# One scaled maximum for two heads: a VectorE multiply and one ScalarE add in place of two ScalarE operations

## The chip, the cores and the metric

The kernel runs on one core of one Trainium2 chip. A core has engines that run side by side, each with its own queue worked off in order: TensorE (PE in the profile; its weight loads are PEld), VectorE (DVE), ScalarE (ACT), GpSimd (POOL) and SyncE (SP), which only starts transfers. The metric is the device time of one execution in microseconds (us). Lower is better.

## What is computed

The program is a two-layer decoder on 16 x 128 = 2048 tokens of width 256: in each layer a self-attention, a cross-attention and a feed-forward part, each followed by a layer norm. The change touches the cross-attention of layer 0 alone. There all 2048 queries attend to all 2048 context rows in 16 heads of dimension 16, and queries, keys, values and the attention weights are rounded to 8 bits:

```python
def _fq_unsigned(x, axis):
    s = jnp.max(x, axis=axis, keepdims=True) / 255.0
    s = jnp.maximum(s, 1e-08)
    q = jnp.clip(jnp.round(x / s), 0.0, 255.0) * s
    return x + jax.lax.stop_gradient(q - x)
...
q = _fq_sym(q, axis=-1)
k = _fq_sym(k, axis=-1)
v = _fq_sym(v, axis=2)
attn = jnp.einsum('bhqd,bhkd->bhqk', q, k)
attn = jax.nn.softmax(attn.astype(jnp.float32), axis=-1)
attn = _fq_unsigned(attn, axis=-1)
out = jnp.einsum('bhqk,bhkd->bhqd', attn, v)
```

The largest weight of a row is that of its largest score. So the 8-bit weight of a score is the rounded value of 255 exp(scale (score - maximum)), which is exp(scale x score + (ln 255 - scale x maximum)). The bracket is one number per query and head. It is this number that the change computes in another way.

## The kernel before

The stage is called joint here because two things run in it together: the cross-attention of layer 0, and, two groups behind it, the feed-forward part of layer 0 for token tiles whose attention is done.

**Steps.** The list `steps` (L1117) has 128 entries (gp, i, u): eight groups gp of two query tiles of 128 tokens, in each group eight head pairs i, for each pair the two tiles u. A group is thus 16 steps. A step takes 128 queries, two heads and 2048 keys. The loop at L1123 runs over the steps, each in two parts, and the order of instructions on PE, DVE, ACT and POOL is the order in which the program writes them (`manual_schedule`, L1122).

**One step, engine by engine.** PE multiplies queries by keys (`scores`, L788), four times two matmuls of 512 keys, into PSUM tiles `s` of which there are two. DVE reads each 128 x 512 block once (`scaled`, L795): it copies the scores into the SBUF tile `e` (four buffers, two a step) and at the same time gives their running maximum; the last of its four entries for a head, `mx[:, 3, hh]`, is the maximum over all 2048 keys for head hh of the pair. That is eight DVE operations a step. ACT then forms the per-query bias of both heads (`exponent`, L812, into the tile `snl`), and one step later writes the 8-bit weights of 2048 keys with one Exp for each head (`weights8`, L827), which reads `e`, the bias from `snl` and the positive scale `qs`. PE turns the weights round, four bytes as one fp32 word (`words_T`, L840, into `aTp`); ACT or DVE copies them to SBUF (`words_out`, L846: by DVE in part 0, by ACT in part 1); POOL spreads the bytes into bf16 (`spread`, L850); PE multiplies them by the values (`context`, L863) in slices that are placed in later steps.

**The scales.** `qs` and its negative `qneg` hold one column for each of the 16 heads of a query tile. POOL computes both in `query_scale` (L616, L618), several steps before the tile's first step.

**The order inside part 1 of step n on the two engines.** DVE: four reductions of step n, then whatever was put off to this place (`due(at, "DVE")`: additions to the residual L899, norm statistics L137 and L138, the query maximum L610 and L612). ACT: copies put off to "ACT first" (L987, L165, L1007), the Exp of head 1 of step n - 1, the copy of the turned words, the feed-forward's tanh and copy (`ffn_out`, L949 and L950), and last `exponent` of step n. The Exp of head 0 of step n follows in part 0 of step n + 1, after the "ACT first" copies of that part where there are any.

**Around it.** Feed-forward matmuls (`ffn_gate` L931, `ffn_down` L966), the query projection of the next group (`query`, L991 to L1007: PE L603, DVE L610 and L612, POOL L616 to L628, PE L635, ACT L1007), and the output projection (L896) are placed at fixed steps of each group by `pair_work` (L1072) and `unit` (L1065). They share one PSUM bank, `misc`.

Of the kernel before, what the change touches and what calls it, by code (L numbers as in the profile page):

```python
# [18 lines left out]
F32 = mybir.dt.float32  # L19
# [3 lines left out]
AF = mybir.ActivationFunctionType  # L23
ALU = mybir.AluOpType
# [3 lines left out]
P = 128  # L28
# [20 lines left out]
def decoder(ctx: ExitStack, tc: tile.TileContext, w: dict, out: bass.AP):  # L49
    nc = tc.nc  # L50

    const = ctx.enter_context(tc.tile_pool(name="const", bufs=1))
    stat = ctx.enter_context(tc.tile_pool(name="stat", bufs=4))
# [157 lines left out]
    with ExitStack() as ph:  # L211
# [14 lines left out]
        wts, bias = {}, {}  # L226
# [291 lines left out]
        states, cks = {}, {}  # L518
# [68 lines left out]
    with ExitStack() as ph:  # L587
# [50 lines left out]
        qs, qneg = {}, {}  # L638
# [127 lines left out]
        ln255 = pool.tile([P, 1], F32, name="ln255")  # L766
# [10 lines left out]
        def group(gp):  # L777
            ssum = stat.tile([P, 2, 16], F32, tag="ssum", name="ssum", bufs=3)
            groups[gp] = ([], ssum)
# [11 lines left out]
        def scaled(gp, i, u, half, c, st, s):  # L791

            quarter = 2 * half + c
            for hh in range(2):
                nc.vector.tensor_scalar(  # L795
                    st["e"][hh][:, half, c * G : (c + 1) * G],
                    s[:, hh, :],
                    1.0,
                    None if quarter == 0 else st["mx"][:, quarter - 1, hh : hh + 1],
                    ALU.mult,  # L800
                    ALU.max,
                    accum_out=st["mx"][:, quarter, hh : hh + 1],
                )
# [4 lines left out]
        def exponent(gp, i, u, st):  # L808

            st["nm"] = stat.tile([P, 2], F32, tag="snl", name="snl")  # L810
            for hh in range(2):
                nc.scalar.activation(  # L812
                    st["nm"][:, hh : hh + 1],
                    st["mx"][:, 3, hh : hh + 1],
                    AF.Identity,
                    bias=ln255,
                    scale=qneg[2 * gp + u][:, 2 * i + hh : 2 * i + hh + 1],
                )

        def weights8(gp, i, u, hh, st):  # L820

# [15 lines left out]
        def words_T(hh, st):  # L837
            pt = ps.tile([P, 4, P], F32, tag="tp", name="aTp", bufs=2)
            for b in range(4):
                nc.tensor.transpose(pt[:, b, :], st["a"][hh][:, b * P : (b + 1) * P], ident)  # L840
            return pt

        def words_out(hh, st, pt, copy):

            at = wk.tile([P, 4, P], F32, tag="at", name="at", bufs=3)
            copy(at.bitcast(U16), pt.bitcast(U16))  # L846
            st["at"][hh] = at
# [126 lines left out]
        states, aTs, os = {}, {}, {}  # L974
# [7 lines left out]
        def later(at, engine, f, *args):  # L982
            put_off.setdefault((at, engine), []).append((f, args))

        def due(at, engine):
            for f, args in put_off.pop((at, engine), []):
                f(*args)  # L987
# [130 lines left out]
        states, aTs, os = {}, {}, {}  # L1118
# [3 lines left out]
        with tc.manual_schedule(engines=set(ordered)):  # L1122
            for n in range(len(steps) + 9):  # L1123
                now = steps[n] if n < len(steps) else None
                if now is not None:
                    if n % 16 == 0:
                        group(n // 16)
                    if n < NB:
                        nc.gpsimd.tensor_tensor(xs[n], xs[n], bp, ALU.add)
                    states[n] = {  # L1130
                        "e": [wk.tile([P, 2, 2 * G], F32, tag="e", name="e", bufs=4) for _ in range(2)],
                        "mx": stat.tile([P, 4, 2], F32, tag="smx", name="smx"),
                        "a": [],
                        "at": {},
                    }
                for part in range(2):
                    at = 2 * n + part
                    if now is not None:
                        if at == 0:
                            waiting = scores(*now, 0, 0)  # L1140
                        scaled(*now, part, 0, states[n], waiting)
                        scaled(*now, part, 1, states[n], scores(*now, part, 1))
                    due(at, "DVE")
                    m = n - 2 + part
                    due(at, "PE")
                    for hh in range(2):

                        q = n - 3 if (n - 3) % 2 == 1 else n - 4
                        turn = (2 * (n - q) + part, hh)

                        if hh == 1 and 0 <= m < len(steps):
                            pt = words_T(1 - part, states[m])
                        if hh == 1 and at + 1 < 2 * len(steps):
                            waiting = scores(*steps[(at + 1) // 2], (at + 1) % 2, 0)
                        if 0 <= q < len(steps) and turn in turns:
                            gp, i, _ = steps[q]
                            if turn == (7, 0) and i % 4 == 0:
                                os[gp, i // 4] = ps.tile([P, 2 * P], F32, tag="o", name="o")
                            o = os[gp, i // 4]
                            context(i, range(*turns[turn]), aTs[gp, i], o)  # L1160
                            if turn == (9, 1):
                                aTs.pop((gp, i))
                                if i % 4 == 3:
                                    later(
                                        at + 1,
                                        "ACT first",
                                        nc.scalar.copy,
                                        ot[:, i // 4],
                                        os.pop((gp, i // 4)).rearrange("p (u q) -> p u q", u=2),
                                    )  # L1170
                                if i == 7 and gp < LAST:
                                    later(at, "DVE last", sums, gp)
                                    for u in range(2):
                                        later(at + 1, "POOL", by_dim, gp, u)
                    if part == 1:
                        unit(n, 1, at)
                    due(at, "ACT first")

                    if 0 <= n - 1 < len(steps):
                        weights8(*steps[n - 1], part, states[n - 1])  # L1180
                    if 0 <= m < len(steps):
                        words_out(1 - part, states[m], pt, nc.scalar.copy if part else nc.vector.tensor_copy)
                    due(at, "ACT")
                    if 0 <= n - 2 < len(steps):
                        gp, i, u = steps[n - 2]
                        if part == 0 and u == 0:
                            aTs[gp, i] = wk.tile([P, NB, 2, 2 * P], BF16, tag="aT", name="aT")
                        due(at, "POOL first")
                        spread(u, part, states[n - 2], aTs[gp, i])
                    due(at, "POOL first")  # L1190
                    due(at, "POOL")
                    if now is not None and part == 1:
                        exponent(*now, states[n])
                    due(at, "DVE last")
                    if (n, part) == (len(steps), 1):
                        later(at + 1, "DVE", sums, LAST)
                        for u in range(2):
                            later(at + 2, "POOL", by_dim, LAST, u)
                    if n < len(steps):
                        pair_work(n, bool(part))  # L1200
                    else:
                        tail_work(n, bool(part))
                if n == len(steps) + 3:
                    ffn_load_all()
                states.pop(n - 3, None)
            assert not put_off, put_off

            for i in range(NI):
                for n in range(2):
                    ffn_gate(LAST, i, n, "s")  # L1210
                th, gu = ffn_tiles(LAST, i, tail=True)
                ffn_out(LAST, th, gu)
                ffn_sigmoid(th, nc.vector)
                ffn_mult(LAST, i, th, gu, nc.vector)
            exp_tables()
            for u in range(2):
                ffn_put_out(LAST, range(NI * u, NI * u + NI), 0, "s")
                due(1, "DVE")
            due(1, "POOL")
            due(2, "POOL first")  # L1220
# [199 lines left out]
    with ExitStack() as ph:  # L1420
# [53 lines left out]
        with tc.manual_schedule(engines={mybir.EngineType.PE, mybir.EngineType.Activation}):  # L1474
# [6 lines left out]
            for h in range(len(halves) + 8):  # L1481
# [16 lines left out]
                if 0 <= h - 2 < len(halves):  # L1498
                    u, d = halves[h - 2]
# [19 lines left out]
    with ExitStack() as ph:  # L1519
# [51 lines left out]
        with tc.manual_schedule(engines={mybir.EngineType.PE}):  # L1571
# [8 lines left out]
            for n in range(len(steps) + 14):  # L1580
# [15 lines left out]
                if 0 <= n - 3 < len(steps):  # L1596
                    u, c = steps[n - 3]
# [135 lines left out]
```

## Time and profile before

| what | value |
|---|---|
| time before, median of 3 runs | 2814.71 us (2813.69 to 2815.48) |
| the profiled execution: its own time | 2814.12 us |
| span of its trace | 2812.4 us |
| joint stage, first to last reduction at L795 | 867.0 to 1718.2 us |
| L812, two to a step | x256, 89.2 us busy, median 392 ns |
| L827, two to a step | x256, 534.8 us busy, mean 2098 ns |
| L795, eight to a step | x768 of mean 745 ns, x256 of mean 682 ns |
| mean granted PE clock | 0.969 |

The profile page has a row for each engine over the span in 40 slices of 70 us; a digit is the busy share in tenths. The joint stage lies in the 13th to 25th slice, and in it DVE and ACT stand at 9 almost throughout while PE stands at 8. Durations of neighbouring instructions of DVE and ACT overlap a little, so the cost of one in a full queue is better read from start to start in the timeline. A busy share over the stage also hides that the stage has stretches with different limits. The page's first table gives for the whole program PE 91%, DVE 72%, ACT 59%, POOL 44%.

### The profile page before, as it was taken

What the parts mean: (1) busy time and instruction counts of PE and PEld (TensorE: products, weight loads), DVE (VectorE), ACT (ScalarE), POOL (GpSimd) and SP (SyncE); (2) the same over time, 40 slices, a digit from 0 to 9 for tenths busy, and PEclk for the clock granted to TensorE, in tenths of its full rate; (3) what the DMA queues carried; (4) which work ended last, traced back from release to release, by engine and by line L of the source; (5) the groups of instructions that cost most, each with busy time, mean ns of one, the idle gap of its engine ahead of it and who ended that gap; (6) DMA issues with size and microseconds to landing.
All of it is one profiled execution on the core that took longest, in us unless ns stands there. A gap on an engine that the chain in (4) does not pass through costs nothing.

```text
span 2812.4 us, 45068 instructions
## 1 busy us (share of the span) xinstructions
PE 2557.1 (91%) x15957; PEld 1594.8 (57%) x15988; DVE 2017.6 (72%) x5525; ACT 1672.6 (59%) x3178; POOL 1236.6 (44%) x1390
## 2 busy tenths in 40 slices
PE   6999999999987788888888888899988899999998
PEld 3677777777753344444444445565655555565646
DVE  5877878777759999999999995577867753333232
ACT  2566566666637999989999996455555442223120
POOL 6544444444446777877778776323322200000000
PEclk9999999999996899999999999999999999999999
DMA  8000000000010000100000001400010011111120
GB/s 242 3 1 1 1 1 1 1 1 1 1 38 10 1 12 20 29 12 22 24 14 26 20 16 51 148 2 2 2 52 12 4 48 58 42 49 53 38 64 12
DMA packets 85009, 79.71 MB, mean 28 GB/s; under 512 B 19728, under 2 KB 66288, under 8 KB 84272
## 3 DMA queue, kind: packets, MB, share of 16 engines
q1 hardware_dynamic: 83520, 73.41, 8.6%
q0 software_dynamic: 1264, 3.42, 0.6%
q8 instruction: 127, 2.08, 0.3%
q14 instruction: 98, 0.80, 0.1%
HBM read 74.57 MB, written 2.23 MB: 27 GB/s over the span
## 4 chain that ended last, share of the span: by engine, by line
PE 66%; DVE 13%; ACT 10%; issue 5%; POOL 4%; DMA 1%; SPq 0%; ACTq 0%; DVEq 0%; POOLq 0%
PE proj L377 11%; PE gate L1641 6%; PE py L1672 6%; PE up L1641 6%; DVE e L795 6%; PE po L507 4%; ACT a L827 4%; PE gu L931 3%; PE o L863 2%; PE sc L423 2%; PE o L1360 2%; PE s L788 2%; PE pm L495 2%; PE aTp L840 2%; PE pm L494 2%
## 5 line engine op out<-in xcount | busy, mean ns | idle before, releaser
L850 POOL CAST aT<-at 128x2048 bf16<-128x2048 uint8 x256 | 482.9, 1893 | 176.0 <-ACT at L846 100.4
L795 DVE TENSOR_SCALAR_CACHE_REDUCE e<-s,smx 128x512 f32<-128x512 f32 x768 | 535.6, 745 | 23.7 <-PE s L788 20.9
L827 ACT ACTIVATE a<-e,snl,qs 128x2048 uint8<-128x2048 f32 x256 | 534.8, 2098 | 0.0
L788 PE MATMUL s<-kT,qT 64*128 64x512 bf16 x1024 | 212.1, 409 | 68.8 <-DVE e L795 67.1
L840 PE MATMUL aTp<-ident,a 128*128 128x128 f32 x1024 | 178.3, 299 | 34.9 <-ACT a L827 34.7
L1645 DVE TENSOR_TENSOR h<-h,up 128x512 f32<-128x512 f32 (+1 forms) x100 | 68.8, 688 | 192.7 <-PE up L1641 191.4
L1644 ACT ACTIVATE h<-gate 128x512 f32<-128x512 f32 (+1 forms) x100 | 59.7, 597 | 220.5 <-PE gate L1641 220.2
L863 PE MATMUL o<-aT,vq 128*32 128x256 bf16 x2048 | 189.4, 289 | 0.0
L795 DVE TENSOR_SCALAR_CACHE_REDUCE e<-s 128x512 f32<-128x512 f32 x256 | 167.1, 682 | 27.6 <-PE s L788 22.1
L1351 ACT COPY prT<-tp 128x512 f32<-128x512 f32 x192 | 104.8, 587 | 123.6 <-PE tp L1350 123.2
L840 PEld LDWEIGHTS aTp<-ident,a 128*128 128x128 f32 x1024 | 114.4, 148 | 99.7 <-ACT a L827 58.6
L1641 PE MATMUL gate<-xT,w_L_ffn_w1g 128*128 128x512 f32 x352 | 167.7, 595 | 0.0
L788 PEld LDWEIGHTS <-qT 64*128 64x128 bf16 x1024 | 56.9, 93 | 194.3 <-issue 193.9
L1641 PE MATMUL up<-xT,w_L_ffn_w1u 128*128 128x512 f32 x352 | 165.4, 592 | 0.0
L1672 PE MATMUL py<-w_L_ffn_w2T,h 128*128 128x256 f32 x704 | 154.6, 379 | 0.0
L846 ACT COPY at<-aTp 128x1024 uint16<-128x1024 uint16 x128 | 129.2, 1010 | 33.8 <-PE aTp L840 32.4
L1316 POOL TENSOR_TENSOR vz<-v,ones 128x1024 f32<-128x1024 f32 (+1 forms) x32 | 58.6, 1831 | 201.1 <-ACT v L1453 83.9
L1339 DVE TENSOR_REDUCE amx<-sc 128x8 f32<-128x1024 f32 x96 | 116.5, 1216 | 38.9 <-PE sc L1331 38.7
L1672 PEld LDWEIGHTS py<-w_L_ffn_w2T,h 128*128 128x128 f32 x704 | 133.7, 190 | 18.3
L377 PE MATMUL proj<-Wlk,xT 128*128 128x512 f32 x256 | 123.7, 606 | 7.4 <-DMA Wlk<-in_L_attn_Wlk 6.3
L447 ACT ACTIVATE pls<-sc,lm,rms_rs 128x128 f32<-128x128 f32 x256 | 113.8, 454 | 25.7 <-DVE lm L443 25.7
L931 PE MATMUL gu<-xT,wgu 128*128 128x256 f32 x448 | 126.6, 405 | 2.4 <-ACT gu_s L950 2.2
(317 smaller groups left out, 5977.8 us busy)
## 6 DMA issues: line engine op xcount, KB each, us to landing
wgu<-in_L_ffn_gu SPq DMA_DIRECT2D x112, 128.0 KB
sh<-share SPq DMA_DIRECT2D x32, 256.0 KB
sh<-share SPq DMA_DIRECT2D x16, 224.0 KB
sh<-share SPq DMA_DIRECT2D x16, 192.0 KB
w_L_ffn_w1g<-in_L_ffn_w1g SPq DMA_DIRECT2D x1, 2816.0 KB
w_L_ffn_w1u<-in_L_ffn_w1u SPq DMA_DIRECT2D x1, 2816.0 KB
w_L_ffn_w2T<-in_L_ffn_w2T SPq DMA_DIRECT2D x1, 2816.0 KB
sh<-share SPq DMA_DIRECT2D x16, 160.0 KB
```

The costliest lines, as they stand in the source:

```text
L377: nc.tensor.matmul(pp.rearrange("p h d -> p (h d)"), lhsT=xTt(b, k), rhs=wts[nm, hg][:, k, :], start=k == 0, stop=k == 1)
L788: nc.tensor.matmul(s[:, hh, :], lhsT=qT[t % 4][r, i, :], rhs=kT[r, i, at : at + G], start=True, stop=True)
L795: nc.vector.tensor_scalar(st["e"][hh][:, half, c * G : (c + 1) * G], s[:, hh, :], 1.0, None if quarter == 0 else st["mx"][:, quarter - 1, ...
L827: nc.scalar.activation(a.bitcast(U8), st["e"][hh].rearrange("p a b -> p (a b)"), AF.Exp, bias=st["nm"][:, hh : hh + 1], scale=qs[2 * gp + ...
L840: nc.tensor.transpose(pt[:, b, :], st["a"][hh][:, b * P : (b + 1) * P], ident)
L846: copy(at.bitcast(U16), pt.bitcast(U16))
L850: nc.gpsimd.tensor_copy(aT[:, :, hh, u * P : (u + 1) * P].rearrange("p (b j) q -> p b j q", j=4), st["at"].pop(hh).bitcast(U8).rearrange(" ...
L863: nc.tensor.matmul(o[r : r + 32], lhsT=vq[:, n, h // 2, h % 2 : h % 2 + 2].rearrange("p w d -> p (w d)"), rhs=aT[:, n, hh], start=n == 0 a ...
L931: nc.tensor.matmul(ffn_ps[q][:, n, :], lhsT=wt[:, k, :], rhs=xT[q // 2][:, k, at], start=k == 0, stop=k == 1)
L1339: nc.vector.tensor_reduce(mx, sc, AX.X, ALU.max)
L1641: nc.tensor.matmul(pp[:rows], lhsT=wt[:, k, :], rhs=xT[g][:, k, :], start=k == 0, stop=k == 1)
L1672: nc.tensor.matmul(py, lhsT=h[:rows, i4 * P : (i4 + 1) * P], rhs=wt, start=n == 0, stop=n == len(parts) - 1)
```

## The change

The multiplication by the negative scale moves from ACT to DVE. DVE does it for both heads in one operation on 128 x 2 numbers, straight after the last reduction of a step and ahead of what was put off to that place. ACT then adds ln 255 to both heads' products in one operation whose scale is a plain number. A new tile `smq` (four buffers) carries the products.

```diff
         def exponent(gp, i, u, st):
 
             st["nm"] = stat.tile([P, 2], F32, tag="snl", name="snl")
-            for hh in range(2):
-                nc.scalar.activation(
-                    st["nm"][:, hh : hh + 1],
-                    st["mx"][:, 3, hh : hh + 1],
-                    AF.Identity,
-                    bias=ln255,
-                    scale=qneg[2 * gp + u][:, 2 * i + hh : 2 * i + hh + 1],
-                )
+            nc.scalar.activation(st["nm"], st["mq"], AF.Identity, bias=ln255)
+
+        def scaled_max(gp, i, u, st):
+            st["mq"] = stat.tile([P, 2], F32, tag="smq", name="smq")
+            nc.vector.tensor_tensor(st["mq"], st["mx"][:, 3, :], qneg[2 * gp + u][:, 2 * i : 2 * i + 2], ALU.mult)
...
                         scaled(*now, part, 1, states[n], scores(*now, part, 1))
+                        if part == 1:
+                            scaled_max(*now, states[n])
                     due(at, "DVE")
```

No matmul and no transfer is added or taken away. The count of ACT operations falls by 128 (256 to 128), that of DVE operations rises by 128.

## The prediction

> **What bounds the kernel now.** I read the page's rows first, then the groups of DVE and ACT instructions, then the chain that ended last, the timeline and the windows. The groups:
>
> ```profile
> L827 ACT ACTIVATE a<-e,snl,qs 128x2048 uint8<-128x2048 f32 x256 | 534.8, 2098 | 0.0
> ...
> L812 ACT ACTIVATE snl<-smx,ln,qneg 128x1 f32<-128x1 f32 x256 | 89.2, 397 | 13.7 <-DVE e L795 13.3
> ...
> L103 ACT ACTIVATE nrs<-nss,eps 128x1 f32<-128x1 f32 x32 | 9.4, 294 | 0.8
> ...
> L443 DVE TENSOR_TENSOR lm<-lm,rms_rs 128x4 f32<-128x4 f32 x64 | 10.4, 162 | 0.0
> ```
>
> The reader is to see the operation that goes (L812), and the two rows nearest to what comes: an ACT operation with a pointer bias but a plain scale (L103, 294 ns), and a small DVE product (L443, 162 ns).
>
> A bare step needs about 5.6 us of ACT and 5.9 us of DVE, so neither wins everywhere. From the third group of steps on, every group takes 109.22 us (for instance 1184.73 to 1293.95 between the same L812), and the chain changes engine inside it. Two pieces of the chain, both from the group that starts at 1184.7:
>
> ```profile
> 1190.37 0.40 ACT th L949
> 1190.76 0.47 ACT gu_s L950
> 1191.23 0.56 ACT snl L812 x2
> 1191.79 2.08 ACT a L827 x2
> 1193.92 0.66 PE aTp L840 x4
> ...
> 1228.99 1.42 DVE e L795 x5
> 1230.41 0.34 DVE x L899
> 1230.78 0.44 DVE ln_st L137
> ```
>
> In the first, ACT sets the pace and the 0.56 us of the L812 pair lies on the chain. In the second, DVE does, and anything put after its eighth reduction lies on the chain. I walked through one group and counted. On the chain are **five L812 pairs** (those at 1266.4, 1272.9, 1286.8, and the two like 1184.9 and 1191.2) and **five ends of a step's reductions on DVE** (1208.4, 1216.1, 1223.5, 1230.4, 1250.5). The rest of the group's chain is PE work, the POOL query rounding and other DVE work.
>
> The first two groups have less PE work: from 867 to 1015 the chain is almost all DVE and passes 19 ends of steps. After the last group's slow PE stretch, from 1688 to 1721, ACT never idles and the chain is ACT alone, with six more pairs.
>
> **The change on ACT.** In the timeline the L812 pair starts at 1191.09 and the Exp behind it at 1191.66, so a pair holds ACT for 0.57 us. The new single operation has one pointer fewer; by the L103 row it lasts 0.295 us. What it holds depends on what follows. If an independent copy follows (L1007, L165 or L987), neighbours overlap: the copy at 1189.46 lasts 1.01 and the next starts at 1190.35, so 0.11 is hidden and the operation holds 0.185; saving 0.385. If the Exp follows directly it reads this very result. Before, it read what the *first* of the pair wrote while the second covered the delay. The row for a result read at once is this:
>
> ```profile
> 1873.42 0.29 ACT L103 ACTIVATE ln_rstd<-ln_mv,eps 128x4 f32<-128x4 f32 x1
> 1873.75 0.20 ACT L104 ACTIVATE ln_rstd<-ln_rstd 128x4 f32<-128x4 f32 x1
> ```
>
> No overlap, 0.33 from start to start; saving 0.24. The Trainium skill ("ScalarE: Activation LUTs", What ACT_TABLE_LOAD costs) prices each pointer operand at about 93 ns, as the rows do, and says that neighbouring ACTIVATEs overlap by about 93 ns, without an exception for a dependent one. By the rule all five pairs of a group save about 0.38, 1.9 us; by the rows it is 3 x 0.24 + 2 x 0.385 = **1.49 us**. I take the rows. If the new operation keeps the old 0.39 us, the saving is 0.98.
>
> **The change on DVE.** The product has no row of its own size; L443 at 162 ns is nearest. It reads what the accumulator read just wrote, and no row shows that wait. Now the next instruction starts together with the read (both at 1230.37). Low end: no wait, 0.16 less the overlap of 0.08: 0.08. Between: read 0.08, a gap of 0.04 as between L137 and L138 (1208.80 + 0.43, then 1209.27), then 0.16, less 0.08: 0.20. High: no overlap afterwards, 0.28. I take **0.20**, as L138 is a dependent small operation of the same engine. Five on a group's chain: 1.0 us. Behind the product in DVE's queue stand the residual additions of L899 and the reductions of the next step; PE waits for both (psum `misc` and `s`).
>
> **The added wait.** ACT now waits for the product, not the maximum, so it gets the bias about 0.2 us later. In the ACT-bound steps DVE has finished 1.4 to 3.4 us before L812 starts, so this is free. In the three or four steps of a group where L812 waits for DVE, ACT idles 0.8 to 1.8 us later in the same step for PE, which itself waits for DVE; that is the cover, and without it the cost would be 0.2 us a step. `qneg` is ready well ahead.
>
> **Sum along the old chain.** First two groups: 19 x 0.20 = +3.8, less 0.4 for one pair; six periods of 1.0 - 1.49 = -0.49: -2.9; the end: 4 x 0.24 + 2 x 0.385 = -1.7. Together -1.2 us, under 0.05%.
>
> **The clock ties this sum.** The granted clock halves once in each group, for two windows of 3.41 us:
>
> ```profile
> 1216.16:1219.57 3.41, 2.06 (x16) 1.00 0.01 2
> ...
> 1229.81:1233.22 3.41, 1.51 (x12) 1.00 0.00 0
> 1233.22:1236.64 3.42, 2.58 (x14) 0.50 0.00 0
> 1236.64:1240.05 3.41, 3.41 (x19) 0.50 0.00 0
> 1240.05:1243.46 3.41, 3.41 (x26) 1.00 0.00 1
> ...
> 1260.53:1263.94 3.41, 1.89 (x20) 1.00 0.13 38
> ```
>
> The columns are the stretch, its length, PE busy with its instructions, and the clock. After a window with PE busy for 1.51 us the clock is 0.50. The windows lie on a fixed grid, and the group's 109.22 us is 32 windows of 3.413 us. That is no accident (from the second group on, the step with L812 at 1047.91 comes again after 109.17, 109.21 and 109.22 us): PE takes over the chain from DVE at 1234.06, inside the slow stretch. Arrive x earlier and x more of the slow stretch is spent on chain work at half rate, which returns x/2. So an early or late arrival decays by half per group until the period is 32 windows again. The Trainium skill ("TensorE: Matmul & The Clock Gate", Why this matters for your kernels) asks for no PE gaps over some 3 us. By that rule the clock would not fall here, the longest gap being 1.3 us, and the plain sum -1.2 would hold. The trace shows it fall after gaps of 0.51 and 1.27 us in one window, so I keep the tie.
>
> With it, the first groups' +3.4 is just one window and persists; the -0.49 of a period is met once, not six times (it moves PE's arrival 0.98 earlier, 0.1 past the stretch's start at 1233.22, so a slow drift may add a few tenths); the end gives -1.7. Total +3.4 - 0.5 - 1.7 = **+1.2 us**. On the profiled execution of 2814.12 us, whose span is 2812.4, this is 2815.3; that execution is 0.6 below the median, so 2815.9 on the median. I forecast **no change** (2816): the difference that a measurement of this kernel can tell is about 0.2%, 5.6 us.
>
> **Rivals.**
>
> *Slower: another window at half clock in each group.* The product's 0.2 us at 1216.1 comes just before the window that starts at 1216.16 and takes PE's busy time there from 2.06 to about 1.86. Those windows of this stage that I asked for and that half clock follows have 1.49 to 1.96; others have 1.97 and more, save two at 1.88 and 1.89. So about 1.9 decides. The window behind it holds 2.11 us of PE work, which does not fit into 3.41 at half rate. Price: 0.8 us there and up to 1.7 where the slow window falls on pure PE chain, as behind 1260.53. Seven times 0.8 to 1.7, with more DVE ends becoming critical beside it: +6 to +12, and with the forecast's +1.2 about **2826**. For it: PE waits for DVE in just this place. Against: the next window's gaps (0.17 and 1.12) cover half of the loss.
>
> *Faster: the product is nearly hidden.* At 0.08 a product and 0.38 a pair, a period gains 1.9 - 0.4 = 1.5, which no arrival inside the slow stretch can return; six periods give -9, the opening +1.1, the end -2.3: about -10, **2805**. For it: small DVE operations do overlap their neighbours. Against: the product depends on the instruction just ahead.
>
> *Not as described:* the compiler could keep a pointer scale of 1.0 on ACT; then savings fall to 0.98 a period, 2817 with the tie.
>
> **Numbers.** No change 0.46 (it includes the last rival), slower 0.32, faster 0.22. The likeliest case alone reaches 2811 to 2820. The range 2807 to 2828 takes in the slow rival up to its upper end and most of the fast one; outside I leave 2 in 10.
>
> **What would show it.** A new DVE row of x128 near 160 ns, with the next instruction starting about 0.2 later than now; an ACT row of x128 near 0.3 us, the Exp 0.33 behind it; the step period in the ACT-bound steps at 6.1 instead of 6.36; groups still 109.2 us long. A group of 111 us or a second half-clock stretch in it would show the first rival, groups below 108 the second. The forecast is wrong if the product costs over 0.3 us on DVE or if slow windows appear or vanish.

## The result, and the profile after

The changed kernel takes 2840.39 us (median of 5 runs) where the kernel before, run beside it, takes 2815.48 us: a ratio of 1.0082, with a 95% interval of 1.0068 to 1.0097. It is slower by 0.8%, some 25 us. The forecast was no change.

The groups of instructions of the changed kernel that answer to the changed lines (line, engine, operation, output and inputs, shapes, count, busy us, mean ns, idle time of the engine just ahead, and what ended it):

```profile
L811 ACT ACTIVATE snl<-smq,ln 128x2 f32<-128x2 f32 x128 | 38.7, 302 | 56.0 <-DVE smq L815 55.2
...
L815 DVE TENSOR_TENSOR smq<-smx,qneg 128x2 f32<-128x2 f32 x128 | 52.1, 407 | 4.4
```

ScalarE's new operation is what was expected (302 ns). The product on VectorE is not: its mean is 407 ns, and ScalarE now idles 55.2 us for it. The mean hides two kinds. The view of the tile `smq` in the same kernel gives shortest, median and longest:

```profile
L815 DVE TENSOR_TENSOR smq<-smx,qneg x128: 160/161/1879, 875.7 to 1742.3; 128x2 f32<-128x2 f32 x128
```

At least half of the products take no more than 161 ns, and single ones more than ten times that. Of the 128 in the timeline, 97 take 0.16 to 0.21 us; the other 31 last over 0.3 us, and together these hold 31.0 us more than 161 ns each. Here is a long one in the timeline of the changed kernel (start and duration in us, engine, line):

```profile
887.13 1.89 POOL L847 CAST aT<-at 128x2048 bf16<-128x2048 uint8 x1
887.15 0.08 DVE L795 DVE_READ_ACCUMULATOR e<-s,smx 128x1 f32 x1
887.26 1.78 DVE L815 TENSOR_TENSOR smq<-smx,qneg 128x2 f32<-128x2 f32 x1
...
888.96 0.68 DVE L795 TENSOR_SCALAR_CACHE_REDUCE e<-s 128x512 f32<-128x512 f32 x1
```

GpSimd's cast starts at 887.13 and ends at 889.02; the product starts 0.13 later and ends at 889.04. Behind it the next reduction starts at 888.96. With a product that does not wait it would have started near 887.4 (0.22 after the accumulator read, as in e9 below). All 31 long products end 0.01 to 0.02 us after the end of a GpSimd cast of L847, and none of the 97 short ones lies wholly within a cast. The reductions do not suffer: they read their one large input from PSUM, and at 745 and 680 ns their means are those of before.

Where the 25 us are is seen by comparing the start of each group's first Exp in the two traces. The difference is 3.7 us at the first group (the stage's first reduction, ahead of any product, is already 3.4 us late), 16.7 at the second, 22.8 from the third to the eighth, and 23.0 at the stage's last Exp. So the first two groups lose 19.0 us, the other six almost nothing, and a further 4.6 of the span's 27.6 us come after the stage. The 3.4 ahead of the stage and the 4.6 behind it stay unexplained, and nothing ties them to the change: e8 and e11 below are one and the same kernel, and their profiles reach the stage's first reduction 2.4 us apart. In the first two groups the long products hold 11.3 and 6.4 us of waiting, in each later group 1.9 to 2.3.

### The profile page after: what moved, and what is told of

It reads as the page before. It is cut to its first block, busy times and chain, and to the rows that moved or that the text cites. A ratio compares the mean times of both kernels' runs of the same rounds, so it can differ in the third digit from the quotient of the medians.

```text
span 2840.0 us, 45099 instructions
## 1 busy us (share of the span) xinstructions
PE 2573.1 (91%) x15988; PEld 1603.2 (56%) x15988; DVE 2069.7 (73%) x5653; ACT 1636.8 (58%) x3050; POOL 1236.5 (44%) x1390
## 4 chain that ended last, share of the span: by engine, by line
PE 65%; DVE 13%; ACT 11%; issue 6%; POOL 3%; SPq 1%; DMA 1%; ACTq 0%; DVEq 0%; POOLq 0%
PE proj L377 11%; PE gate L1640 6%; PE py L1671 6%; PE up L1640 6%; DVE e L795 6%; ACT a L824 5%; PE po L507 4%; PE gu L928 2%; PE sc L423 2%; PE o L1359 2%; PE o L860 2%; PE pm L495 2%; PE pm L494 2%; PE s L788 2%; PE tp_qk L412 2%
## 5 line engine op out<-in xcount | busy, mean ns | idle before, releaser
L847 POOL CAST aT<-at 128x2048 bf16<-128x2048 uint8 x256 | 482.6, 1891 | 191.6 <-DVE at L843 106.6
L795 DVE TENSOR_SCALAR_CACHE_REDUCE e<-s,smx 128x512 f32<-128x512 f32 x768 | 535.1, 745 | 13.6 <-PE s L788 11.9
```

What stands on the lines that cost most here:

```text
L795: nc.vector.tensor_scalar(st["e"][hh][:, half, c * G : (c + 1) * G], s[:, hh, :], 1.0, None if quarter == 0 else st["mx"][:, quarter - 1, ...
L847: nc.gpsimd.tensor_copy(aT[:, :, hh, u * P : (u + 1) * P].rearrange("p (b j) q -> p b j q", j=4), st["at"].pop(hh).bitcast(U8).rearrange(" ...
```

## The experiments

All ratios are to the kernel before, run beside each on the same chip, with 95% intervals.

### One product, three kinds of input

The first question was whether any small operation at this place costs the time (called the queue theory), or only one that has two inputs in SBUF and therefore waits for GpSimd's cast (called the port theory). Three kernels keep the old form on ScalarE and add to VectorE an operation whose result nobody reads. They differ only in that operation:

```diff
+        def scaled_max(gp, i, u, st):
...
# e2
+            nc.vector.tensor_tensor(st["mq"], st["mx"][:, 3, :], qneg[2 * gp + u][:, 2 * i : 2 * i + 2], ALU.mult)
# e3
+            nc.vector.tensor_reduce(st["mq"], st["mx"][:, 3, :], AX.X, ALU.max)
# e9, with s the last score tile, in PSUM
+            nc.vector.tensor_tensor(st["mq"], st["mx"][:, 3, :], s[:, :, G - 1], ALU.mult)
```

> The kernel before, with the VectorE product added and its result unused; ScalarE keeps its two operations with the pointer scale. Port theory: 16 to 25 products of 0.3 to 1.9 us in the first two groups and a time of 2836 to 2846 us, as in the changed kernel. A theory that ScalarE's longer wait for the bias costs the time: 2813 to 2818 us, as before, since ScalarE waits for nothing new.

> The kernel before, with a small VectorE reduction of the same two maxima (one SBUF input, result unused) in the product's place. Port theory: the reduction lasts 0.1 to 0.2 us in all 128 places, time 2814 to 2823 us. Queue theory: as slow as with the product, 2836 us or more.

> The kernel before, with an unused VectorE product of the same size at the same place, the maxima times one column of the last score tile, so one input in SBUF and one in PSUM. It differs from the dead product in where its second input lies. Port theory: all 128 at 0.15 to 0.2 us, 2824 to 2834 us as with the dead reduction. If a tensor_tensor waits for GpSimd whatever its inputs: single ones of 0.5 to 1.9 us and 2840 us or more.

Measured: 2846.62 us for e2 (ratio 1.0113, 1.0098 to 1.0128), 2829.75 for e3 (1.0049, 1.0032 to 1.0065), 2831.72 for e9 (1.0052, 1.0036 to 1.0067). The rows of the three operations, each from its kernel's groups:

```profile
L822 DVE TENSOR_TENSOR smq<-smx,qneg 128x2 f32<-128x2 f32 x128 | 56.7, 443 | 4.4
```

```profile
L822 DVE TENSOR_REDUCE smq<-smx 128x1 f32<-128x2 f32 x128 | 19.8, 155 | 4.4
```

```profile
L822 DVE TENSOR_TENSOR smq<-smx,s 128x2 f32<-128x2 f32 x128 | 20.0, 156 | 4.4
```

e2 and e9 run the same operation at the same place, and only the second input's memory differs: 443 ns with it in SBUF, 156 ns (longest 158) with it in PSUM. Here is e9's operation at the place where the changed kernel's waited:

```profile
886.30 1.89 POOL L854 CAST aT<-at 128x2048 bf16<-128x2048 uint8 x1
886.32 0.08 DVE L795 DVE_READ_ACCUMULATOR e<-s,smx 128x1 f32 x1
886.43 0.16 DVE L822 TENSOR_TENSOR smq<-smx,s 128x2 f32<-128x2 f32 x1
886.54 0.69 DVE L795 TENSOR_SCALAR_CACHE_REDUCE e<-s 128x512 f32<-128x512 f32 x1
```

It runs through in the middle of a cast, as 34 of e9's 128 operations and 37 of e3's do. The wait is thus for reading SBUF twice while GpSimd works, not for VectorE's own pipeline. It is worth about 17 us in these kernels: each against the kernel before beside it, e2 loses 32.4 us, e3 15.5 and e9 15.4. Those 15 us are the price of one more small operation on VectorE when ScalarE gives nothing back, the clock's answer to it included (see the rivals below). Neither theory had that price right for e3: its time lies between the two ranges. e2 lies 0.6 us above its range, e9 inside. ScalarE's waiting for a later bias is not needed for the loss, since e2 has none.

### ScalarE's part alone

```diff
-            for hh in range(2):
-                nc.scalar.activation(
...
+            nc.scalar.activation(st["nm"], st["mx"][:, 3, :], AF.Identity, bias=ln255, scale=0.0)
```

> ScalarE's part alone: one operation for both heads with a plain scale of 0, so the bias is ln 255 and the maximum is not subtracted; no product on VectorE. What the part saves by itself: 0.24 to 0.385 us in a ScalarE-bound step. With the clock's tie (groups stay 32 windows of 3.413 us): 2809 to 2814 us. Without it (1.5 us in each of six groups and the end): 2802 to 2807 us. If one late operation for both heads costs more than two early ones: 2816 us or more.

This kernel leaves out the subtraction of the maximum, so it is of use for its time alone. Measured: 2805.49 us, 0.9964 (0.9951 to 0.9977). The median lies in the range without the clock's tie. The timeline of this kernel, ScalarE alone:

```profile
1188.34 0.31 ACT L811 ACTIVATE snl<-smx,ln 128x2 f32<-128x2 f32 x1
1188.68 2.09 ACT L820 ACTIVATE a<-e,snl,qs 128x2048 uint8<-128x2048 f32 x1
```

The single operation holds ScalarE for 0.34 us from start to start, against 0.57 for the pair: 0.23 saved where the Exp follows at once. In this profile the groups from the third on take 106.2 to 107.7 us instead of 109.2, so the clock's tie did not hold, and at the stage's last Exp the kernel is 14 us ahead, though it had entered the stage 2.6 late.

### Which groups pay

```diff
# e5: the changed form where this holds, the old form elsewhere; e6: the reverse
+            if 16 * gp + 2 * i + u < 32:
+                nc.scalar.activation(st["nm"], st["mq"], AF.Identity, bias=ln255)
+                return
```

> The changed form in the first two groups (steps 0 to 31) only, the old form in the other 96 steps. Theory that the first two groups lose the time, where 17.7 us of products wait for the GpSimd cast on a chain that is VectorE alone, and that the clock's tie holds the later groups at 32 windows: 2835 to 2843 us, all of the loss. If the loss is spread evenly over the 128 steps: a quarter of it, about 2821 us.

> The old form in the first two groups, the changed form in steps 32 to 127. Theory of the first two groups and the tie: 2808 to 2818 us, although each of these groups still has 2.3 us of waiting products. Spread evenly: about 2833 us.

Measured: e5 2839.54 us (1.0087, 1.0070 to 1.0104), e6 2819.95 us (1.0016, 1.0006 to 1.0025). The first quarter of the steps carries the loss: 24.9 us in e5 against 5.3 in e6. e6 still has 17 long products with 13.6 us of waiting. In its profile it is 2.7 us behind the kernel before at its last Exp and was 3.1 behind at its first, so nothing is lost in the stage. Its median of 2820 lies just above the range; that excess is not explained by this stage.

### The multiplication without the second stream

```diff
# e7
-            nc.vector.tensor_tensor(st["mq"], st["mx"][:, 3, :], qneg[2 * gp + u][:, 2 * i : 2 * i + 2], ALU.mult)
+            for hh in range(2):
+                nc.vector.tensor_scalar(
+                    st["mq"][:, hh : hh + 1],
+                    st["mx"][:, 3, hh : hh + 1],
+                    qneg[2 * gp + u][:, 2 * i + hh : 2 * i + hh + 1],
+                    None,
+                    ALU.mult,
+                )
# e12: e7's form where gp < 2, the changed kernel's product elsewhere
```

> The product as two operations of one column each, with the negative scale as a per-partition pointer, so that only one input streams from SBUF; ScalarE's one addition as in the changed kernel. Port theory, if a pointer does not need the shared read port: none over 0.3 us, VectorE busy 0.3 to 0.35 us longer a step, 2816 to 2828 us. If a pointer needs the port too: single ones of 0.5 to 1.9 us and 2835 us or more. Queue theory (a small dependent operation costs the time, whatever its inputs): two are worse than one, 2845 us or more.

> The changed kernel with one thing undone in steps 0 to 31: there the product is two operations with a pointer scale, which do not wait for GpSimd; from step 32 on it is the changed kernel's one product with two SBUF inputs. Theory that the waits of the first two groups are the loss: 2813 to 2822 us. If the loss comes from VectorE's added work there, or from ScalarE's single late operation: 2835 us or more.

Measured: e7 2812.14 us (0.9989, 0.9980 to 0.9999), e12 2821.64 us (1.0009, 0.9999 to 1.0018; the kernel before took 2819.38 beside it). e7's operations, from the view of its tile:

```profile
L816 DVE TENSOR_SCALAR smq<-smx,qneg x256: 200/210/218, 872.7 to 1716.3; 128x1 f32<-128x1 f32 x128
```

e7 is faster than its range of 2816 to 2828, and e12 lies in its own. Two operations of 210 ns, none longer than 218 though some 50 of the 256 lie wholly within a cast, are cheaper than one of 161 that sometimes waits. And they fit the queue better, as this piece of e12's timeline shows:

```profile
887.28 0.09 DVE L795 DVE_READ_ACCUMULATOR e<-s,smx 128x1 f32 x1
887.28 0.34 DVE L817 TENSOR_SCALAR smq<-smx,qneg 128x1 f32<-128x1 f32 x2
887.53 0.68 DVE L795 TENSOR_SCALAR_CACHE_REDUCE e<-s 128x512 f32<-128x512 f32 x1
```

Both together delay the next reduction by 0.25 us. The first of them needs the maximum of head 0, which was ready one reduction earlier, so it starts together with the last accumulator read. Together with e9, e12 settles the cause: it replaces the product with two SBUF inputs in the first 32 steps of the changed kernel and keeps ScalarE's single late operation, and the first two groups then lose 4.2 us instead of 19.0 (from +3.9 at the first Exp to +8.1 at the third group).

### A version that beats both

e7 suggests going on: the same VectorE operation can add ln 255 too, so that ScalarE has nothing to do. e8 and e11 do that in all steps. e10 does it only where ScalarE sets the pace, and keeps the old pair elsewhere:

```diff
# e8, e11
+            st["nm"] = stat.tile([P, 2], F32, tag="snl", name="snl")
+            for hh in range(2):
+                nc.vector.tensor_scalar(
+                    st["nm"][:, hh : hh + 1],
+                    st["mx"][:, 3, hh : hh + 1],
+                    qneg[2 * gp + u][:, 2 * i + hh : 2 * i + hh + 1],
+                    math.log(255.0),
+                    ALU.mult,
+                    ALU.add,
+                )
# e10: only where
+            if gp > 1 and (2 * i + u < 4 or 2 * i + u == 9 or 2 * i + u > 10):
```

> As the run before, but the two VectorE operations also add ln 255, and ScalarE's operation is gone. ScalarE saves a further 0.2 to 0.33 us in its own stretches: 0 to 12 us faster than the run before, 2806 to 2826 us. If what counts is VectorE's queue alone, the same as the run before.

> The bias wholly on VectorE (two operations, none on ScalarE) only where ScalarE sets the pace: from the third group on, in steps 0 to 3, 9 and 11 to 15 of a group; the old form elsewhere. Theory that each form pays in its own stretch: 2795 to 2803 us, 2 to 8 us faster than with the bias wholly on VectorE in all steps. If the clock's windows take the gain back: within 2 us of that kernel.

> The bias wholly on VectorE in all steps once more, on the same chip as the run before, for comparison: 2801 to 2808 us.

Measured: e8 2804.32 us (0.9960, 0.9945 to 0.9975), e11 2803.05 us (0.9949, 0.9932 to 0.9966), e10 2799.01 us (0.9935, 0.9920 to 0.9949). e8 is 1.7 us faster than its range; e10 and e11 lie in theirs. e10 is the fastest kernel of this study, by 0.65% over the kernel before. It is 4 us under e11 on the same chip, as the count of which engine sets the pace in which step had it; the intervals of the two ratios overlap a little, but each of e10's four times lies below each of e11's. In e11's profile the first two groups lose 3.7 us and the rest gains; in e10's the first two groups lose nothing.

### One that tested something else

> The change as it is, but the negative scales of a query tile are copied once per tile (16 small DVE copies in all) into unused PSUM, so that the product has one input in SBUF and one in PSUM. Port theory (the product waits because its two SBUF inputs need the read port that a GpSimd cast holds): no product longer than 0.3 us, products 0.16 to 0.25 us, time 2811 to 2823 us. Queue theory (a small dependent operation at this place of VectorE's queue costs this much whatever its inputs): products still up to 1.8 us or the time still 2835 us or more.

The copies went into the free half of the PSUM tile that `context` fills (`oq[:, 0:256]` for the output, `oq[:, 256:320]` for the scales). It took 3134.85 us (1.1135, 1.1119 to 1.1152). The view of who waited for the product says most of why:

```profile
L824 DVE TENSOR_TENSOR smq<-smx,oq x128: 156/157/158, 875.5 to 2037.1; 128x2 f32<-128x2 f32 x128
...
  PE oq L869: 254.2, 110
```

The products were all short, as the port theory has it. But the value matmuls waited 254.2 us for them, since both now used the same tile. The time says nothing on the question; e9 replaced this run.

## Why the prediction was wrong, point by point

**The term that failed is the price of the product on VectorE**, set at 0.20 us, between 0.08 and 0.28. Unhindered it was right: in e9 the next reduction starts 0.22 us after the accumulator read (886.32 and 886.54), in e3 0.23. In e12, with 0.25, the first two groups lose 4.2 us where I had +3.8 for VectorE less 0.4 for ScalarE. But I bounded the cost by what stands in VectorE's queue alone and put nothing for GpSimd. The product reads two tiles from SBUF, and 31 of 128 times it waited for a cast, 1.0 us in the mean and 1.7 at most. The bound from above was short by nearly a whole cast. Instead of +3.4 the opening cost 19.0.

The trace of before held a warning that I did not read. The row that I took for the price, L443, is itself a product of two SBUF tiles, and the first attention has larger ones; their views give shortest, median and longest:

```profile
L443 DVE TENSOR_TENSOR lm<-lm,rms_rs x64: 139/144/679, 45.6 to 784.0; 128x4 f32<-128x4 f32 x64
L297 DVE TENSOR_TENSOR raw_Wlk<-rope_a,rope_b x64: 414/937/1037, 32.3 to 769.6; 128x256 f32<-128x256 f32 x64
L297 DVE TENSOR_TENSOR raw_Wq<-rope_a,rope_b x64: 414/416/1246, 32.6 to 773.9; 128x256 f32<-128x256 f32 x64
```

L297 is the same operation on the same shape, with a median of 416 ns in one call and 937 in the other. At 100.12 it takes 0.93 us while GpSimd works from 100.05 to 100.78; at 103.48 it takes 0.42 with GpSimd idle, and so (0.41 to 0.42) do all 58 of the second call that meet no GpSimd work. L443 shows the same: 56 of its 64 meet no GpSimd work and take at most 147 ns, and the five that take 272 to 679 ns all end 0.01 to 0.02 us after a GpSimd operation. So the nearest row was well chosen; its mean of 162 ns hid the two kinds. The Trainium skill ("SBUF — State Buffer", Who interferes with whom) states this: a VectorE instruction with two SBUF inputs contends with a GpSimd instruction that reads SBUF, and the one that comes second waits until the first is done. The runs here agree, with 31 ends within 0.02 us of a cast's end. This rule spoke against the change, and it is the one that I should have weighed.

**ScalarE's saving on one pair was right.** I had 0.33 us from start to start with the Exp following; the changed kernel has 0.34 (1213.90 to 1214.24 in its timeline). The Exp that reads the result at once does not overlap it. What a whole group gains was counted low: 1.49 us, where e4's groups from the third to the seventh are 1.6 to 3.0 us shorter, the three shortest with one window at half clock instead of two.

**The clock's tie was right where it was applied, and narrower than I wrote.** The changed kernel's groups from the third on take 109.2 us again, although each has 2.3 us of waiting products and 0.23 us less ScalarE work in many steps. The half-clock stretch comes once a group, as before (stretch, length, PE busy, clock, DMA share, GB/s):

```profile
1147.80:1154.70 6.90, 5.51 (x28) 0.51 0.01 2
1154.70:1257.10 102.40, 88.92 (x626) 1.00 0.08 22
1257.10:1263.90 6.80, 5.51 (x28) 0.50 0.00 0
```

A start 19 us later changed nothing in what follows. e5 even shows the decay by half that I had derived: its third to seventh groups, of the old form behind a late start, take 109.48, 109.36, 109.29, 109.26 and 109.25 us, and their excess over 109.22 about halves each time. But the lock is not firm. e6 runs the changed kernel's program in these groups, and they take 108.9 us with one of 110.3 among them. When a group's work changes by more, the tie lets go: groups of e3, with an operation added, take 109.8 to 111.5 us, and those of e4, with one removed, 106.2 to 107.7. Nor does the border of about 1.9 us that I named decide sharply: over all windows of the stage before, those that half clock followed have up to 1.96 us of PE work, and six that it did not follow have 1.83 to 1.91. That the clock's windows are what ties the groups is thus argued from these times; no run changed the clock alone.

**The rivals.** The slower one named 2826 us and a second half-clock window in each group. In the changed kernel the direction was right, the mechanism was not: the later groups have one stretch each as before, and they lose nothing. In e3 and e9, where ScalarE gives nothing back, the mechanism did come. Here is the slow part of e3's fourth group, which takes 111.5 us (columns as above):

```profile
1231.16:1237.98 6.82, 6.27 (x28) 0.50 0.00 0
1237.98:1244.81 6.83, 4.76 (x36) 1.00 0.01 2
1244.81:1251.64 6.83, 6.43 (x33) 0.50 0.00 0
```

The fifth group has a single stretch and takes 109.8 us: the second costs 1.7, the upper end of the price that I had given it. In the first two groups, for which my "once in each group" does not hold, the clock falls several times already before the change, and more often after it: the mean granted between 872 and 969 us goes from 0.80 to 0.70, and from 969 to 1066 us from 0.90 to 0.81. PE waits longer for VectorE there. In e12, without those waits, it is 0.76 and 0.88, so the fall goes with the waits; how much of the lost time is PE at half clock is not separated. The faster rival did not come, nor the one in which the compiler keeps the pointer.

**The added wait** of ScalarE was held to be covered. In e2, where ScalarE waits for nothing new, the loss is no smaller, so it is not what costs. Of the signs that I had named, groups of 109.2 us and ScalarE-bound steps of 6.1 us came true (6.16 and 6.14 in the steps after 1207.74); the next instruction about 0.2 us later came true in three steps of four and failed in the fourth.

## What to carry to other kernels

Price an added operation by all that it shares, not by its engine's queue alone: for VectorE ask where each input lies and what GpSimd does at that moment, and look in the trace for a row with the same kinds of input, even of another size. Read its shortest, median and longest, not the mean alone: here durations of two kinds (median 161 ns, mean 407) were the sign of a wait for another engine. Before moving work from one engine to another, mark which engine sets the pace in which stretch; the move pays in one kind and costs in the other, and can be made for one kind only, as e10 does.

## What the runs showed of the hardware

Two things were not expected. A per-partition pointer scale on VectorE (one number per partition, on one column of data) does not count as a second SBUF input: 256 such operations in e7, amid the same casts, stay within 200 to 218 ns, while a product of two SBUF tiles goes up to 1.88 us. And in this stage the half clock needed no long gap: it followed single windows of 3.41 us in which PE was busy for about half (1.51 us before, 1.81 in the changed kernel's later groups), though not every such window. The loop that hands over to PE inside the slow stretch kept to 32 of these windows a group so closely, in the changed kernel, that a delay of 19 us in the first groups is carried through the six that follow within 0.3 us; in e6, with the same later groups, it kept to them only in the mean.
